# Attention followed by a quantised conv block: small products cut in halves, loads for the next block moved, and a count moved between conv bands

## The chip, the cores and the metric

One core of a Trainium2 chip runs one program. The metric is the device time of that program in microseconds, from its first to its last instruction, the median of several runs. All engine, line and tile names are those of the profile: PE is the matmul unit (TensorE), DVE is VectorE, ACT is ScalarE, POOL is GpSimd, SP is SyncE, which here only issues transfers.

## The reference

The input x has 4 images of 128 channels and 64 x 64 pixels, in float32. Two layers follow one another:

```python
# layer 0: attention over the 4096 pixels of an image, 4 heads of 32 channels
x_norm = group_norm(x, norm_w, norm_b)                      # 8 groups
qkv = einsum('oc,bchw->bohw', qkv_w, x_norm) + qkv_b
q, k, v = heads(qkv)                                        # [4, 4, 4096, 32] each
attn = softmax(einsum('bhid,bhjd->bhij', q, k) * 32**-0.5)
out = einsum('bhij,bhjd->bhid', attn, v)
x = x + einsum('oc,bchw->bohw', proj_w, out) + proj_b
# layer 1: two 3x3 convolutions with 3-bit weights, batch norm over all images
out = relu(batchnorm(conv3x3(x, lsq_quantize(w1, alpha1))))
out = batchnorm(conv3x3(out, lsq_quantize(w2, alpha2)))
x = relu(out + x)
```

## The kernel before

**Blocks and steps.** The attention runs as 32 blocks, `n` from 0 to 31: image `b` = n // 8 and a chunk `qb` = n % 8 of 512 queries. A block takes 32 steps `kt`, each over 128 keys. A step's scores are two pairs of heads; a pair (L418, tile s, two PSUM banks, three such tiles in turn) is four matmuls, and ACT takes its exponential (L420) into the tile p, of which there are eight. `weights` (L431) multiplies p by v into the accumulator acc (four matmuls, which the profile counts as eight; so are those of the small products). The sum of p over the keys, needed for softmax, is gathered by DVE (L441, L443) into r for 26 of the 32 steps; for the steps 4, 9, 14, 19, 24 and 28 (`MOVED`) a transfer of POOL adds p into rm instead (L436, L438), and one more adds rm to r (L464, `merge`).

**Order of the work.** It is written out by hand. The loop alternates a short phase (three pairs of scores, then one step of weights) and a long phase (three pairs, then two steps); both make a period of three steps. Every engine runs its instructions in that order. After the weights of step kt, `side(kt)` emits the tasks that `schedule(n, before)` has put at kt or earlier. `slots` lists the steps of a block that end a short phase: every third, 10 or 11 a block.

**Small products.** These are the tasks that use TensorE: for the next image, the projections k, q and v of a 512-pixel chunk j (`project_parts`, products pk, pq, pv at L301); for the block before, the sums l (`total`, L460) and the output projection po (L301). Each fills one PSUM bank of the pool `psa`. That pool has two buffers and acc holds one of them, so a small product can begin only when the one before it has been emptied. pk and pq are emptied by ACT (L331) and then DVE (L332), which split the value in two parts in a staging tile; POOL then writes that tile to DRAM (L336). pv is emptied by DVE (L350), l by ACT (L468), po by DVE (L516). In the first block the projections of image 0 that aren't made ahead of the loop are tasks too: 16 products in steps 0 to 23, in short and in long phases.

**The end of a block.** `merge`, `sums` (l), `spread`, `invert`, `gather`, `weigh` and `project` follow one another in the next block: l is copied to SBUF, row sums are spread over partitions by a transfer (lq), DVE inverts them (rq, L496), a transfer writes them to DRAM (rd) and another broadcasts them (rc), DVE multiplies (`weigh`, L506), TensorE projects (po), DVE adds the residual x (`store`, L516) and POOL writes y.

**Loads.** SP issues, in program order, the loads of x chunks (L230, three buffers), of q for the next block (L398, eight transfers, two buffers), of k and v for the next image (L387, L391, in the last quarter block of an image), and the transfers lq, rd and rc. In a block with qb = 1 the statistics for the next image's group norm are taken: eight x chunks are loaded at steps 0, 2, ... 14 and DVE runs bn_stats (L628) three steps later; then come the small products gm, gv and gb with DVE work between them (`norm_parts`).

**The convolutions** (`conv`, L701) run over 16 bands of 16 rows, each as 2 x 18 products from a high and a low part of the input (`split_band`, DVE, L541 and L542). ACT copies a result from PSUM to cv (L761) and DVE takes bn_stats of the copy (L762). Ahead of band 2 the kernel counts sums that were too large: two DVE instructions (L724, L726), a product of one column (nbad, L728) and a copy to cnt (L729).

Of the kernel before, what the change touches and what calls it, by code (L numbers as in the profile page):

```python
# [78 lines left out]
def _fast_body(ctx, tc, x, norm_w, norm_b, qkv_wt, qkv_b, proj_wt, proj_b,  # L79
# [223 lines left out]
    def project_parts(b, j, xin, start=False):  # L303
# [19 lines left out]
        def mm(what, o):  # L323
            ps[what] = bank(what)
            banded(ps[what], norm[b][0][:, o : o + P], xin())
# [12 lines left out]
        def mmv():  # L338
            ps["v"] = bank("v")
            for i in range(KB):  # L340
                banded(ps["v"][:, i * P : (i + 1) * P], xin()[:, i * P : (i + 1) * P],
                       norm[b][0][:, 2 * P : 3 * P])

        def evac_v():
# [8 lines left out]
            if b > 0:  # L353
                nc.gpsimd.dma_start(out=vd[b, j], in_=v)

        return [lambda: mm("k", P), lambda: parts("k", 0, kd),
                lambda: mm("q", 0), lambda: parts("q", 1, qd), mmv, evac_v]
# [87 lines left out]
    def finish_parts(n):  # L445
# [10 lines left out]
        def total(r, first, end):  # L456
            if first:
                t["l"] = psa.tile([P, FB], F32, name=f"l{n}", tag="a")
            for h in range(HEADS):
                nc.tensor.matmul(t["l"][h * D : (h + 1) * D, :], ones, r[:, h, :],  # L460
                                 start=first, stop=end)
# [8 lines left out]
        def sums():  # L470
            total(rsum[n], True, True)
            evacuate()
# [93 lines left out]
    def first_chunk(j, what, start):  # L566
        fs = project_parts(0, j, lambda: halves[j // 4][:, j % 4, :], start)
        i = 2 * "kqv".index(what)
        return fs[i : i + 2]
# [13 lines left out]
    late = {}  # L583

    def schedule(n, before):
        b, qb = blocks[n]
        todo = []
        slots = [kt for kt in range(NK - 1) if (n * NK + kt) % 3 == 0]

        def add(kt, f):  # L590
            todo.append((kt, f))

        if before:
            add(1, before["merge"])
            kt = slots[3]
            add(kt, before["sums"])
            add(kt + 1, before["spread"])
            add(kt + 3, before["invert"])
            add(kt + 4, before["gather"])
            add(kt + 6, before["residual"])  # L600
            add(kt + 11, before["weigh"])
            add(slots[8], before["project"])
            add(slots[8] + 1, before["store"])
        if n + 1 < len(blocks) and qb < NB - 1:
            add(14, lambda: load_q(b, qb + 1))
        if b + 1 < B and qb == NB - 1:
            add(24, lambda: load_q(b + 1, 0))

        def chunk(kts, fs):
            for i, kt in enumerate(kts):  # L610
                add(kt, fs[2 * i])
                add(kt + 1, fs[2 * i + 1])

        if n == 0:
            for kt, what, j in ((0, "v", 3), (2, "q", 1), (3, "k", 4), (5, "q", 2), (6, "k", 5),
                                (8, "q", 3), (9, "k", 6), (11, "v", 4), (12, "k", 7), (14, "v", 5),
                                (15, "v", 6), (17, "v", 7), (18, "q", 4), (20, "q", 5),
                                (21, "q", 6), (23, "q", 7)):
                chunk((kt,), first_chunk(j, what, False))
                if what == "k":  # L620
                    add(kt + 2, lambda j=j: load_k(0, j))
        if b + 1 < B:
            if qb == 1:
                st = small.tile([P, NB, 6], F32, name=f"st{b + 1}", tag="st")
                xs = {}
                for j in range(NB):
                    add(2 * j, lambda j=j: xs.update({j: load_x(b + 1, j)}))
                    add(2 * j + 3, lambda j=j: nc.vector.bn_stats(st[:, j, :], xs[j]))  # L628
                late[b] = norm_parts(b + 1, st)
                add(18, late[b][0])  # L630
                chunk((slots[7], slots[9]), late[b][1:5])
            if qb == 2:
                chunk(slots[0:1], late[b][5:7])
            for j, i in {2: ((0, (1, 2, 4)), (1, (5, 6, 7))), 3: ((2, (1, 2, 4)), (3, (5, 6, 7))),
                         4: ((4, (4, 5, 6)),), 5: ((5, (4, 5, 6)),), 6: ((6, (4, 5, 6)),),
                         7: ((7, (4, 5, 6)),)}.get(qb, ()):
                xt = {}
                kts = [slots[i] for i in i]
                add(max(kts[0] - 8, 0), lambda j=j, xt=xt: xt.update({0: load_x(b + 1, j)}))
                chunk(kts, project_parts(b + 1, j, lambda xt=xt: xt[0]))  # L640
# [81 lines left out]

    big = small.tile([P, 1], F32, name="big")
    nc.vector.tensor_reduce(big, worst, AX.X, ALU.max)  # L724
    bad = small.tile([P, 1], F32, name="bad")
    nc.vector.tensor_scalar(bad, big, LIMIT, None, ALU.is_gt)  # L726
    nbad = psa.tile([P, FB], F32, name="nbad", tag="a")
    nc.tensor.matmul(nbad[0:1, 0:1], bad, ones[:, 0:1], start=True, stop=True)  # L728
    nc.vector.tensor_copy(cnt, nbad[0:1, 0:1])  # L729
# [19 lines left out]
    def layer(i, prepare, done):  # L749

        st = mid.tile([P, B * NB, 6], F32, name=f"st{i}")
        for m, (b, g) in enumerate(bandlist):
# [5 lines left out]
            for j in range(2):  # L758
                c = 2 * g + j
                dst = cv[b][:, c * FB : (c + 1) * FB]  # L760
                nc.scalar.copy(dst, ps[:, j, :])  # L761
                nc.vector.bn_stats(st[:, b * NB + c, :], dst)  # L762
        return batch_norm(i, st)

    def first(m):
        if m + 3 < len(bandlist):
            load_band(*bandlist[m + 3])
# [513 lines left out]
```

## Time and profile before

| | us |
|---|---|
| time, median of 3 | 2655.54 (2654.3 to 2663.69) |
| span of the profiled run | 2654.6 |
| first scores to the first copy av<-acc (block 0) | 29.8 to 141.7 |
| block 1, copy to copy | 79.4 |
| block 9, copy to copy | 82.4 |
| last copy av<-acc, end of the attention | 2329.8 |

The copies av<-acc (L453), one at the end of each block, mark the blocks in time. Work of the engines in some blocks, from the stretches that these copies bound (us busy):

| stretch | PE | DVE | ACT |
|---|---|---|---|
| 29.8 to 141.7 (block 0) | 91.17 | 66.97 | 70.66 |
| 141.7 to 221.1 (block 1) | 70.46 | 62.56 | 60.40 |
| 715.3 to 797.8 (block 9) | 71.42 | 63.57 | 63.10 |
| 575.6 to 646.4 (block 7) | 69.34 | 60.49 | 61.86 |
| 2265.0 to 2329.8 (block 31) | 64.80 | 60.27 | 57.47 |

A row of the groups reads: line, engine, operation, output<-input with their shapes, count, then busy time and mean ns of one, then the time for which the engine stood idle ahead of them and what ended it. In the chain of waits each row is a start, a length and the work (or transfer) that the end was waiting for at that moment.

### The profile page before, as it was taken

The numbers are of one execution on the slowest core, as the hardware profiler recorded it, in microseconds if no ns is written. First come the engines' busy times: TensorE is split into PE (matmuls) and PEld (weight loads), VectorE is DVE, ScalarE is ACT, GpSimd is POOL, SyncE is SP. The second block draws the span as 40 slices with busy tenths as digits, with TensorE's granted clock in tenths as the row PEclk, the third lists the DMA queues.
The fourth block names the chain that finished last, engine by engine and source line by source line (L and its number), as shares of the span: only waits on it lengthen the run. The fifth ranks groups of instructions, "written<-read, shape, count | busy, mean of one in ns | idle before, by whom it ended". The sixth has DMA issues, their size and how long they took to land.

```text
span 2654.6 us, 46871 instructions
## 1 busy us (share of the span) xinstructions
PE 2543.2 (96%) x19634; PEld 1193.5 (45%) x19634; DVE 2134.9 (80%) x1402; ACT 2075.5 (78%) x2275; POOL 282.1 (11%) x456
## 2 busy tenths in 40 slices
PE   5889999999989999999999999999999999999995
PEld 2334444444434444443444444444444444467773
DVE  4678889888878888888988888878999999954334
ACT  3678888888878888888888888888898989911223
POOL 2101111111001111111011111110001001000000
PEclk9999999999999999999999999999999999999997
DMA  4765666778766666678766766796656667744004
GB/s 156 179 147 140 164 157 156 163 185 203 164 137 164 175 153 154 153 192 190 166 152 173 170 160 164 157 224 148 140 126 150 138 140 152 142 85 148 0 0 160
DMA packets 147411, 399.94 MB, mean 151 GB/s; under 512 B 59240, under 2 KB 60008, under 8 KB 118648
## 3 DMA queue, kind: packets, MB, share of 16 engines
q0 software_dynamic: 45888, 280.59, 46.3%
q1 hardware_dynamic: 100728, 115.23, 16.8%
q8 instruction: 156, 2.56, 0.4%
q10 hardware_dynamic: 576, 1.05, 0.1%
q14 instruction: 63, 0.52, 0.1%
HBM read 105.32 MB, written 55.83 MB: 61 GB/s over the span
## 4 chain that ended last, share of the span: by engine, by line
PE 85%; DMA 6%; issue 3%; DVE 2%; ACT 1%; POOL 0%; SPq 0%; POOLq 0%; ACTq 0%; DVEq 0%
PE s L418 38%; PE acc L431 33%; PE c L701 9%; DMA rm<-p 3%; DMA q<-qd 1%; PE l L460 1%; DVE r L443 1%; PE po L301 1%; PE pq L301 1%; PE pk L301 1%; PE pv L301 1%; DMA x<-in_x_dram 1%; DVE res L819 0%; ACT p L420 0%; DMA v<-vd 0%
## 5 line engine op out<-in xcount | busy, mean ns | idle before, releaser
L420 ACT ACTIVATE p<-s 128x1024 f32<-128x1024 f32 x2048 | 1932.0, 1034 | 302.0 <-PE s L418 228.1
L443 DVE TENSOR_TENSOR r<-r,p 128x2048 f32<-128x2048 f32 x768 | 1758.1, 2289 | 118.0 <-ACT p L420 72.7
L418 PE MATMUL s<-q,k 64*128 64x512 f32 x8192 | 1181.1, 416 | 12.4 <-ACT p L420 4.5
L418 PEld LDWEIGHTS s<-q,k 64*128 64x128 f32 x8192 | 709.2, 186 | 734.7 <-ACT p L420 322.6
L431 PE MATMUL acc<-p,v 128*32 128x512 f32 x8192 | 1023.6, 602 | 0.0
L431 PEld LDWEIGHTS acc<-p,v 128*32 128x32 f32 x8192 | 197.6, 109 | 456.0 <-issue 451.7
L438 POOL DMA_DIRECT2D rm<-p x160 | 139.3, 871 | 912.0 <-ACT p L420 674.6
L761 ACT COPY cv<-c 128x512 f32<-128x512 f32 x64 | 34.3, 590 | 223.8 <-PE c L701 210.8
L762 DVE BATCH_NORM_STATS2 st<-cv 128x6 f32<-128x512 f32 x64 | 41.2, 685 | 154.9 <-ACT cv L761 154.9
L701 PE MATMUL c<-hi,wq 128*128 128x512 f32 x576 | 151.4, 408 | 6.6 <-DVE hi L780 6.6
L701 PE MATMUL c<-lo,wq 128*128 128x512 f32 x576 | 148.0, 401 | 0.0
L701 PEld LDWEIGHTS c<-hi,wq 128*128 128x128 f32 x576 | 110.4, 192 | 38.0 <-issue 8.7
L701 PEld LDWEIGHTS c<-lo,wq 128*128 128x128 f32 x576 | 108.7, 189 | 29.1
L441 DVE TENSOR_TENSOR r<-p,p 128x2048 f32<-128x2048 f32 x32 | 73.3, 2290 | 42.9 <-ACT p L420 42.6
L332 DVE SCALAR_TENSOR_TENSOR kst<-pk,b,kst 128x512 fp32r<-128x512 f32 x32 | 24.0, 751 | 81.5 <-ACT kst L331 81.4
L332 DVE SCALAR_TENSOR_TENSOR qst<-pq,b,qst 128x512 fp32r<-128x512 f32 x32 | 24.0, 749 | 39.3 <-ACT qst L331 39.3
L464 POOL DMA_DIRECT2D r<-rm x31 | 26.3, 849 | 240.1 <-DMA rm<-p 108.4
L628 DVE BATCH_NORM_STATS2 st<-x 128x6 f32<-128x512 f32 x24 | 16.5, 687 | 32.9 <-DMA x<-in_x_dram 32.9
L336 POOL DMA_DIRECT2D kd<-kst x28 | 20.8, 744 | 205.3 <-DVE kst L332 191.0
L336 POOL DMA_DIRECT2D qd<-qst x31 | 23.1, 745 | 183.3 <-DVE qst L332 183.1
L436 POOL DMA_DIRECT2D rm<-p x32 | 17.8, 556 | 225.6 <-ACT p L420 140.0
L517 POOL DMA_DIRECT2D y<-x x32 | 18.5, 577 | 195.3 <-DVE x L516 195.3
(129 smaller groups left out, 660.1 us busy)
## 6 DMA issues: line engine op xcount, KB each, us to landing
rm<-p POOLq DMA_DIRECT2D x192, 1024.0 KB, 7.6
q<-qd SPq DMA_DIRECT2D x248, 128.0 KB
r<-rm POOLq DMA_DIRECT2D x31, 1024.0 KB, 7.0
x<-in_x_dram SPq DMA_DIRECT2D x80, 256.0 KB
k<-kd SPq DMA_DIRECT2D x124, 128.0 KB
qd<-qst POOLq DMA_DIRECT2D x31, 512.0 KB, 4.5
kd<-kst POOLq DMA_DIRECT2D x28, 512.0 KB, 6.1
y<-x POOLq DMA_DIRECT2D x32, 256.0 KB, 3.2
```

The source lines that it names most:

```text
L301: nc.tensor.matmul(out[cs, :], w[:, cs], x, start=True, stop=True)
L332: nc.vector.scalar_tensor_tensor(lo, ps[what], bias, t[:, 0, :], ALU.add, ALU.subtract)
L336: (nc.sync if start else nc.gpsimd).dma_start(out=dst[b, j].rearrange("s p n -> p s n"), in_=t)
L418: nc.tensor.matmul(s[:, i, :], k[r, half, c0 : c0 + P], q[r, half, part, :], start=(part == 0), stop=(part == 1))
L420: nc.scalar.activation(pts[step][:, 2 * half : 2 * half + 2, :], s, AF.Exp, scale=SCALE)
L431: nc.tensor.matmul(acc[n][h * D : (h + 1) * D, :], v[:, kt % KB, h * D : (h + 1) * D], pt[:, h, :], start=(kt == 0), stop=(kt == NK - 1))
L438: nc.gpsimd.dma_start(out=msum[n], in_=pt, accum_op=ALU.add)
L441: nc.vector.tensor_tensor(rsum[n], pts[step - 1], pt, ALU.add)
L443: nc.vector.tensor_tensor(rsum[n], rsum[n], pt, ALU.add)
L701: nc.tensor.matmul(ps[:, j, :].rearrange("p (r w) -> p r w", w=W), w[:, tap, :], part[:, j * RB + kh : j * RB + kh + RB, kw : kw + W], sta ...
L761: nc.scalar.copy(dst, ps[:, j, :])
L762: nc.vector.bn_stats(st[:, b * NB + c, :], dst)
```

## The change

- The small products k, q, v and l are cut in two halves of 256 columns. A helper `visit` puts the halves at the two slots that it is given (or both at one slot, as one product in two parts) and the emptying one step after the second. In blocks with one chunk, k goes to slots 0 and 1, l to 3 and 4, q to 5 and 6, v to 7 and 8; po moves from slot 8 to slot 9, and weigh to two steps ahead of it. In blocks with two chunks (qb 2 and 3) only the second v is cut.
- In the first block ten products are left, most of them three steps apart; six q products move to block 1.
- The x chunks for the statistics are loaded every one and a half steps, the x chunk of a block's first projection in the block before (step 22), and q for the next block is always loaded at step 14, across images too.
- The count of bad sums moves from ahead of band 2 to band 5, and bn_stats in the conv layers reads the result in PSUM, before the copy.

It is meant to spread the small products over the short phases, and to keep loads clear of what waits for them.

```diff
--- before.py
+++ after.py
@@ -320,9 +320,13 @@
                 t = stage.tile([P, n, FB], F32, name=f"{what}st{b}_{j}", tag=tag)
             return t
 
-        def mm(what, o):
-            ps[what] = bank(what)
-            banded(ps[what], norm[b][0][:, o : o + P], xin())
+        halves = [slice(i * FB // 2, (i + 1) * FB // 2) for i in range(2)]
+        def mm(what, o, i):
+            if i == 0:
+                ps[what] = bank(what)
+            cs = halves[i]
+            banded(ps[what][:, cs], norm[b][0][:, o : o + P], xin()[:, cs])
 
         def parts(what, o, dst):
             t = staged(2, what)
@@ -335,9 +339,10 @@
             else:
                 (nc.sync if start else nc.gpsimd).dma_start(out=dst[b, j].rearrange("s p n -> p s n"), in_=t)
 
-        def mmv():
-            ps["v"] = bank("v")
-            for i in range(KB):
+        def mmv(i):
+            if i == 0:
+                ps["v"] = bank("v")
+            for i in range(i * KB // 2, (i + 1) * KB // 2):
                 banded(ps["v"][:, i * P : (i + 1) * P], xin()[:, i * P : (i + 1) * P],
                        norm[b][0][:, 2 * P : 3 * P])
 
@@ -353,8 +358,10 @@
             if b > 0:
                 nc.gpsimd.dma_start(out=vd[b, j], in_=v)
 
-        return [lambda: mm("k", P), lambda: parts("k", 0, kd),
-                lambda: mm("q", 0), lambda: parts("q", 1, qd), mmv, evac_v]
+        return dict(k=(lambda: mm("k", P, 0), lambda: mm("k", P, 1), lambda: parts("k", 0, kd)),
+                    q=(lambda: mm("q", 0, 0), lambda: mm("q", 0, 1), lambda: parts("q", 1, qd)),
+                    v=(lambda: mmv(0), lambda: mmv(1), evac_v))
 
 
     def k_tile(b, j):
@@ -453,11 +460,11 @@
             nc.scalar.copy(av, acc[n])
 
 
-        def total(r, first, end):
-            if first:
+        def total(r, first, end, cs=slice(0, FB)):
+            if "l" not in t:
                 t["l"] = psa.tile([P, FB], F32, name=f"l{n}", tag="a")
             for h in range(HEADS):
-                nc.tensor.matmul(t["l"][h * D : (h + 1) * D, :], ones, r[:, h, :],
+                nc.tensor.matmul(t["l"][h * D : (h + 1) * D, cs], ones, r[:, h, cs],
                                  start=first, stop=end)
 
         def merge():
@@ -467,9 +474,10 @@
             t["ls"] = stage.tile([P, FB], F32, name=f"ls{n}", tag="ls")
             nc.scalar.copy(t["ls"], t["l"])
 
-        def sums():
-            total(rsum[n], True, True)
-            evacuate()
+        def sums(i):
+            total(rsum[n], True, True, slice(i * FB // 2, (i + 1) * FB // 2))
+            if i == 1:
+                evacuate()
 
 
         def sums_at_once():
@@ -564,9 +572,7 @@
         f()
 
     def first_chunk(j, what, start):
-        fs = project_parts(0, j, lambda: halves[j // 4][:, j % 4, :], start)
-        i = 2 * "kqv".index(what)
-        return fs[i : i + 2]
+        return project_parts(0, j, lambda: halves[j // 4][:, j % 4, :], start)[what]
 
     def load_kv(b, j):
         load_k(b, j)
@@ -580,64 +586,79 @@
 
 
 
-    late = {}
+    late, xin = {}, {}
+    def fetch(b, j):
+        xin[b, j] = load_x(b, j)
 
...
         slots = [kt for kt in range(NK - 1) if (n * NK + kt) % 3 == 0]
+        two = b + 1 < B and qb in (2, 3)
+        full = two or n == 1
 
         def add(kt, f):
             todo.append((kt, f))
 
+        def visit(kts, first, second, evacuate=None):
+            add(kts[0], first)
+            add(kts[-1], second)
+            if evacuate:
+                add(kts[-1] + 1, evacuate)
         if before:
             add(1, before["merge"])
-            kt = slots[3]
-            add(kt, before["sums"])
+            kts = slots[3:4] if full else slots[3:5]
+            visit(kts, lambda: before["sums"](0), lambda: before["sums"](1))
+            kt = kts[-1]
             add(kt + 1, before["spread"])
             add(kt + 3, before["invert"])
             add(kt + 4, before["gather"])
             add(kt + 6, before["residual"])
-            add(kt + 11, before["weigh"])
-            add(slots[8], before["project"])
-            add(slots[8] + 1, before["store"])
-        if n + 1 < len(blocks) and qb < NB - 1:
-            add(14, lambda: load_q(b, qb + 1))
-        if b + 1 < B and qb == NB - 1:
-            add(24, lambda: load_q(b + 1, 0))
-        def chunk(kts, fs):
-            for i, kt in enumerate(kts):
-                add(kt, fs[2 * i])
-                add(kt + 1, fs[2 * i + 1])
+            add(slots[9] - 2, before["weigh"])
+            add(slots[9], before["project"])
+            add(slots[9] + 1, before["store"])
+        if n + 1 < len(blocks):
+            add(14, lambda: load_q(*blocks[n + 1]))
         if n == 0:
-            for kt, what, j in ((0, "v", 3), (2, "q", 1), (3, "k", 4), (5, "q", 2), (6, "k", 5),
-                                (8, "q", 3), (9, "k", 6), (11, "v", 4), (12, "k", 7), (14, "v", 5),
-                                (15, "v", 6), (17, "v", 7), (18, "q", 4), (20, "q", 5),
-                                (21, "q", 6), (23, "q", 7)):
-                chunk((kt,), first_chunk(j, what, False))
+            for kt, what, j in ((0, "k", 4), (2, "q", 1), (3, "v", 3), (6, "k", 5), (9, "k", 6),
+                                (12, "v", 4), (15, "k", 7), (18, "v", 5), (21, "v", 6),
+                                (24, "v", 7)):
+                visit((kt,), *first_chunk(j, what, False))
                 if what == "k":
                     add(kt + 2, lambda j=j: load_k(0, j))
+        if n == 1:
+            for i, j in zip((0, 1, 2, 4, 5, 6), range(2, NB)):
+                visit(slots[i : i + 1], *first_chunk(j, "q", False))
         if b + 1 < B:
             if qb == 1:
                 st = small.tile([P, NB, 6], F32, name=f"st{b + 1}", tag="st")
-                xs = {}
                 for j in range(NB):
-                    add(2 * j, lambda j=j: xs.update({j: load_x(b + 1, j)}))
-                    add(2 * j + 3, lambda j=j: nc.vector.bn_stats(st[:, j, :], xs[j]))
+                    add(3 * j // 2, lambda j=j: fetch(b + 1, j))
+                    add(3 * j // 2 + 3, lambda j=j: nc.vector.bn_stats(st[:, j, :], xin[b + 1, j]))
                 late[b] = norm_parts(b + 1, st)
-                add(18, late[b][0])
-                chunk((slots[7], slots[9]), late[b][1:5])
+                add(15, late[b][0])
+                for i in (0, 1):
+                    add(slots[7 + i], late[b][1 + 2 * i])
+                    add(slots[7 + i] + 1, late[b][2 + 2 * i])
             if qb == 2:
-                chunk(slots[0:1], late[b][5:7])
-            for j, i in {2: ((0, (1, 2, 4)), (1, (5, 6, 7))), 3: ((2, (1, 2, 4)), (3, (5, 6, 7))),
-                         4: ((4, (4, 5, 6)),), 5: ((5, (4, 5, 6)),), 6: ((6, (4, 5, 6)),),
-                         7: ((7, (4, 5, 6)),)}.get(qb, ()):
-                xt = {}
-                kts = [slots[i] for i in i]
-                add(max(kts[0] - 8, 0), lambda j=j, xt=xt: xt.update({0: load_x(b + 1, j)}))
-                chunk(kts, project_parts(b + 1, j, lambda xt=xt: xt[0]))
+                add(slots[0], late[b][5])
+                add(slots[0] + 1, late[b][6])
+            chunks = {1: (), 2: (0, 1), 3: (2, 3), 4: (4,), 5: (5,), 6: (6,), 7: (7,)}
+            for i, j in enumerate(chunks.get(qb, ())):
+                p = project_parts(b + 1, j, lambda j=j: xin[b + 1, j])
+                if not two:
+                    places = dict(k=slots[0:2], q=slots[5:7], v=slots[7:9])
+                elif i == 0:
+                    places = dict(k=slots[1:2], q=slots[2:3], v=slots[4:5])
+                else:
+                    places = dict(k=slots[5:6], q=slots[6:7], v=slots[7:9])
+                    add(8, lambda j=j: fetch(b + 1, j))
+                for what, kts in places.items():
+                    visit(kts, *p[what])
+            if qb > 0 and qb + 1 in chunks:
+                add(22, lambda j=chunks[qb + 1][0]: fetch(b + 1, j))
             if qb == NB - 1:
                 for j in range(NB - 1):
                     add(4 * j + 1, lambda j=j: load_kv(b + 1, j))
@@ -719,14 +740,6 @@
     last["project"]()
     last["store"]()
     split_band(*bandlist[2])
-    big = small.tile([P, 1], F32, name="big")
-    nc.vector.tensor_reduce(big, worst, AX.X, ALU.max)
-    bad = small.tile([P, 1], F32, name="bad")
-    nc.vector.tensor_scalar(bad, big, LIMIT, None, ALU.is_gt)
-    nbad = psa.tile([P, FB], F32, name="nbad", tag="a")
-    nc.tensor.matmul(nbad[0:1, 0:1], bad, ones[:, 0:1], start=True, stop=True)
-    nc.vector.tensor_copy(cnt, nbad[0:1, 0:1])
     att.close()
 
     mid = ctx.enter_context(tc.tile_pool(name="mid", bufs=1))
@@ -758,11 +771,23 @@
             for j in range(2):
                 c = 2 * g + j
                 dst = cv[b][:, c * FB : (c + 1) * FB]
+                nc.vector.bn_stats(st[:, b * NB + c, :], ps[:, j, :])
                 nc.scalar.copy(dst, ps[:, j, :])
-                nc.vector.bn_stats(st[:, b * NB + c, :], dst)
         return batch_norm(i, st)
 
+    def count_bad():
+        big = small.tile([P, 1], F32, name="big")
+        nc.vector.tensor_reduce(big, worst, AX.X, ALU.max)
+        bad = small.tile([P, 1], F32, name="bad")
+        nc.vector.tensor_scalar(bad, big, LIMIT, None, ALU.is_gt)
+        nbad = psa.tile([P, FB], F32, name="nbad", tag="a")
+        nc.tensor.matmul(nbad[0:1, 0:1], bad, ones[:, 0:1], start=True, stop=True)
+        nc.vector.tensor_copy(cnt, nbad[0:1, 0:1])
     def first(m):
+        if m == 5:
+            count_bad()
         if m + 3 < len(bandlist):
             load_band(*bandlist[m + 3])
         if m + 2 < len(bandlist) and m > 0:
```

## The prediction

> **What bounds the kernel now.** I read the busy table first, then the total waits, then the timeline of one ordinary stretch, then the chain of waits in the stretches that run long. The busy table:
>
> ```profile
> PE 2543.2 (96%) x19634; PEld 1193.5 (45%) x19634; DVE 2134.9 (80%) x1402; ACT 2075.5 (78%) x2275; POOL 282.1 (11%) x456
> ```
>
> TensorE sets the end, so the question is which of its gaps the change closes. An ordinary stretch of block 5 in the timeline (start, length, engine, line; TensorE alone):
>
> ```profile
> 556.27 1.67 PE L418 MATMUL s<-q,k 64*128 64x512 f32 x12
> ...
> 558.75 1.04 PE L301 MATMUL po<-av,wp 128*32 128x512 f32 x8
> ...
> 559.72 1.66 PE L418 MATMUL s<-q,k 64*128 64x512 f32 x12
> ...
> 563.17 1.67 PE L418 MATMUL s<-q,k 64*128 64x512 f32 x12
> ...
> 565.76 1.82 PE L418 MATMUL s<-q,k 64*128 64x512 f32 x12
> ...
> 569.37 1.66 PE L418 MATMUL s<-q,k 64*128 64x512 f32 x12
> ```
>
> Every L418 row opens a phase of three score pairs. The short phase has one step of L431 after them, the long phase two. With a small product (po) in the short phase a period is 559.72 - 556.27 = 3.45 plus 563.17 - 559.72 = 3.45, so **6.90 us**. Without one it is 2.59 + 3.61 = **6.20 us**. The product costs 0.70 and not its own 0.86 (3.45 - 2.59), because an empty short phase is paid back: its 2.59 is less than ACT's three exponentials (2.86 on their row), and the next long phase waits for PSUM (3.61 against 3.45). That wait, in total, and two others:
>
> ```profile
> PEld s L418 <- ACT p L420: 322.6, 492, 2.6
> ...
> PE gm L249 <- DVE mv L244: 33.1, 3, 13.6
> ...
> DVE st L628 <- DMA x<-in_x_dram: 32.9, 3, 15.0
> ```
>
> The copies av<-acc (L453), one a block, show which blocks run long: about 66 us in image 3, 69 to 74 with projections, but 79.4 in block 1 and 82.4 in block 9, and block 0 has 111.9 from its first scores to its copy. The chain in block 1:
>
> ```profile
> 171.46 5.85 DMA rd<-rq
> 177.31 0.02 issue
> 177.32 0.59 SPq L503
> 177.91 0.06 issue
> 177.97 0.03 SPq L398
> 178.00 0.04 issue
> 178.04 6.58 DMA q<-qd
> 184.62 0.02 issue
> 184.63 9.02 DMA x<-in_x_dram
> 193.65 0.02 issue
> 193.67 0.04 DVE st L628
> ```
>
> The last x chunk for the statistics is issued behind eight q loads on SyncE's queue; VectorE sits in bn_stats until it lands, and TensorE sits in the gm product. In block 0 the timeline shows another wait: products come one and a half steps apart, through one free psa bank, and each waits until VectorE has emptied it:
>
> ```profile
> 53.42 1.06 PE L301 MATMUL pq<-xh,wn 128*32 128x512 f32 x8 [1.52 <-DVE kst L332]
> ...
> 59.46 1.72 PE L301 MATMUL pk<-xh,wn 128*32 128x512 f32 x8 [2.39 <-DVE qst L332]
> ```
>
> **What the Trainium skill says.** (1) "TensorE: Matmul & The Clock Gate", section Back-to-back issue gap: for wide products the time goes with the columns streamed. The trace agrees: pv is 16 products of 128 columns and occupies 25.4/24 = 1.06 us a chunk, pk is 4 of 512 and occupies 25.0/24 = 1.04. So I price half a product at half of 0.86. (2) Same page, section What's actually happening: an idle window of about 3.4 us drops the clock to half. Agreed: after 3.4 us of idle before the nbad product the next nine matmuls take 3.86 us, against 2.3 elsewhere. (3) "DMA: Bandwidth & Descriptors", section Issuing engines are not separate DMA queues: all transfers share 16 engines. The rm<-p additions, which GpSimd issues, land in 6.9 to 15.2 us here, so moving q loads can slow them. (4) "PSUM — Partial Sum Buffer", section PSUM bank collisions raise a hardware error: two engines must not touch a bank at once; no run shows it yet, but it means the new bn_stats and the copy take turns.
>
> **The change, part by part.**
> - *Halves.* 12 blocks (quarters 4 to 7 of images 0 to 2) halve k, q and v: 36. Six full blocks halve the second v: 6. The l product is halved in 31 - 7 = 24 blocks. That is 66. A product and an empty period cost 6.90 + 6.20 = 13.10 now. In halves a short phase is 2.59 + 0.43 = 3.02, more than 2.86, so the long phase needs no wait: 2 x (3.02 + 3.45) = 12.94. 0.16 to 0.18 each, **-11**. Against it: weigh now comes two steps ahead of the po product, not four. Between them TensorE has about 4.3 us (two weights steps, three pairs, one step); an addition (2.29), weigh (0.69) and v's evacuation (0.68) make 3.7 plus VectorE's lag, which over the additions at steps 25 to 27 has medians of 0.2 to 1.1 us. Some po products wait 0.3 us or so, and block boundaries where store now comes one step before the next acc also: +2. Net **-9**.
> - *Block 0.* 16 products become 10, all but one in short phases three steps apart. The stalls beyond the phases' own work, summed over that window by comparing each phase with ordinary ones, are 27 us after the pipeline has filled. k4 at step 0, q1 at 2, v3 at 3 still crowd: two waits of 2 to 3 us remain. **-22**. Six q products leave (6 x 0.86 = **-5.2**) for block 1. v5 is now made two steps ahead of its use; its evacuation needs one addition and 0.68 us within 4.3 us, so I cost it at nothing. The k staging tile is rewritten 6.9 us apart while its write lands in 6.1 after GpSimd's issue: a wait of about 1 us on ACT, inside its 0.59 of slack a phase.
> - *Block 1.* It gets the six q products (+5.2) and loses the wait of 14 us on x. TensorE then has about 71.5 us. VectorE has 62.6 busy now and gets six evacuations of 0.75: 67, denser in its first half, so it lags. I take 74 against 79.4: **-5.4**.
> - *Blocks 9 and 17.* The loads come at 0, 1, 3 ... 10 with the last bn_stats at 13, ahead of the q loads. Block 9 loses 14 us to its wait and falls to about 70: **-12.5**. Block 17 loses 2.6 now: **-1**. The gather of rc is now issued behind the q loads there and in other blocks; it has from step 14 to weigh at 25 to 27, some 25 us, for q loads (5.5 to 13.4), rd (5.85 with its issue) and rc itself. Hidden.
> - *Image boundaries.* q of the next image is loaded at step 14, not 24. Phases at these three boundaries lose 14.6 us in all; the 6.4 in block 23 are a wait on that load (DMA q<-qd 9.01 in its chain), the rest mostly on rm<-p additions, which stay. **-6**.
> - *Count of bad sums.* TensorE idles 3.4 us before nbad. Band 2's hi is ready at 2351.64, nbad ran at 2353.48: 1.9 saved, and without so long a gap the slow nine matmuls give up to 1.5. bn_stats from PSUM takes turns with the copy: the tail of a layer goes from 1.9 to about 2.1 us, twice. **-3**.
>
> Sum: -9 - 22 - 5.2 - 5.4 - 12.5 - 1 - 6 - 3 = -64.1, so 2655.5 - 64.1 = 2591.
>
> **Rivals.** *A: only the removed waits pay.* Halves give nothing since po and ACT's evacuations (0.70 in a phase with 0.59 of slack) take it back, boundaries stay, block 1 becomes VectorE's: -22 - 5.2 - 3 - 12 - 1 = -43, 2612. For it: VectorE is at 93% in blocks with projections; against it: those blocks show no wait on it now. *B: everything is recovered.* 27 + 12.9 + 14.3 + 2.6 of stalls in blocks 0, 1, 9 and 17, 14.6 at boundaries, 11 for halves, 4 at the bands: -86, 2569. Against it: the crowd at steps 0 to 3 and the rm<-p chain remain. *C: a new wait replaces the old one, and it ends slower.* If rc, rd or lq lands behind the q loads too late, VectorE stops at weigh or invert as it stops at bn_stats now, but in some 22 blocks. At 5 us each that is +110 against -64: 2700. Against it: 25 us of room against at most 22.
>
> **How the numbers follow.** Forecast 0.62, A 0.22, B 0.11, C 0.05. The forecast's own terms are uncertain by about 12 us together, A's centre is 2612 and B's 2569; 2575 to 2617 leaves out C, half of B and the upper third of A, some 2 in 10. Slower is C without its mild form, 0.04; mild forms of C give no change, 0.03; faster 0.93.
>
> **What would show it.** Right: block 0 near 85 us from its first scores to its copy, no wait of bn_stats on x, blocks 1 and 9 at 74 and 70, periods of 6.47 us with 256-column products, TensorE's wait on ACT in L418 down by a third, and no 3.4 us gap ahead of band 2. Wrong: halves that last over 0.5 us, waits of po on VectorE over 1 us, waits of VectorE at weigh or invert on DMA, or a longer rm<-p chain in blocks 7, 15 and 23.

## The result and the profile after

| | before | after |
|---|---|---|
| time, us (median) | 2656.65 (4 runs) | 2589.17 (2588.28 to 2592.37, 4 runs) |
| ratio | | 0.9744, interval 0.9723 to 0.9765 |
| span of the profiled run, us | 2654.6 | 2588.2 |
| first scores to the copy, block 0 | 111.9 | 85.8 |
| block 1 / block 9 | 79.4 / 82.4 | 74.3 / 69.8 |

Since one copy av<-acc ends each block, two profiles can be subtracted block by block. In blocks that an edit doesn't touch the length repeats within 0.3 us from run to run, mostly within 0.1, except for the lead-in and block 0 (up to 2.6 us together), block 1 (up to 1.9) and, now and then, one of 16 to 28 (up to 1.6); from the last copy to the end it repeats within 0.8. The table sets the prediction's terms against these differences.

| term of the prediction | predicted | measured, us |
|---|---|---|
| block 0 (waits, and six q products gone) | -27.2 | -26.9 at its copy |
| block 1 | -5.4 | -5.1 |
| block 9 / block 17 | -12.5 / -1 | -12.7 / -1.1 |
| boundaries (7, 8, 15, 16, 23), beyond halves | -6 | -12.9 |
| halves, gross | -11 | -11.6 |
| what the halves' layout costs (weigh, store) | +2 | +6.4 in blocks 25, 26 and 28 |
| convolutions | -3 | -2.6 |
| sum | -64.1 | -66.4 |

The row of the halves is a remainder: what the blocks that no other row names lost (9.2), with 2.4 added for the halves in the five boundary blocks.

The busy line of the page after: TensorE is busy for a larger share of a shorter span.

```profile
PE 2517.2 (97%) x20394; PEld 1223.4 (47%) x20394; DVE 2140.3 (83%) x1402; ACT 2081.9 (80%) x2275; POOL 281.4 (11%) x456
```

The timeline of block 4 after, TensorE's rows that open a phase, and the half product pk between them (L425 is what L418 was):

```profile
411.35 1.67 PE L425 MATMUL s<-q,k 64*128 64x512 f32 x12
413.83 0.62 PE L301 MATMUL pk<-x,wn 128*32 128x256 f32 x8
414.37 1.66 PE L425 MATMUL s<-q,k 64*128 64x512 f32 x12
417.81 1.67 PE L425 MATMUL s<-q,k 64*128 64x512 f32 x12
420.41 1.89 PE L425 MATMUL s<-q,k 64*128 64x512 f32 x12
```

A short phase with a half lasts 3.02 us and the long one behind it 3.44: together 6.46, and the prediction worked out 6.47. The row at 417.81 opens an empty short phase (2.60), and the scores that follow at 420.41 are stretched to 1.89 by the wait for PSUM. The total waits after:

```profile
PEld s L425 <- ACT p L427: 209.2, 376, 2.0
...
PE gm L249 <- DVE mv L244: 13.6, 1, 13.6
...
PEld po L301 <- DVE av L514: 8.5, 5, 3.4
```

The wait of the scores on ACT is down from 322.6 us, by a third; the one wait of gm that is left is image 0's, ahead of all blocks; bn_stats (L639) waits for x no more. New is the last line: po waits for weigh. In block 0 the timeline still shows the crowd of its first three steps:

```profile
41.29 1.07 PE L301 MATMUL pq<-xh,wn 128*32 128x256 f32 x16 [1.52 <-DVE kst L336]
...
47.33 1.25 PE L301 MATMUL pv<-wn,xh 128*32 128x128 f32 x32 [2.38 <-DVE qst L336]
```

The second of these waits costs more than its 2.38 us. A row of the next view is a stretch and its length, then the busy time of PE, PEld, DVE, ACT and POOL, TensorE's granted clock (1.00 is full) and the load of the transfers. Two pairs of stretches after the change, in block 0 and in block 26:

```profile
44.70:48.11 3.41, 1.03 (x32) 0.78 (x32) 1.81 (x2) 1.79 (x3) 0.54 (x1) 1.00 0.48 151
48.11:51.52 3.41, 3.41 (x28) 2.02 (x24) 1.39 (x2) 1.76 (x2) 0.76 (x2) 0.50 0.89 334
1918.62:1922.03 3.41, 0.89 (x12) 0.16 (x8) 3.41 (x3) 1.12 (x2) 0.00 (x0) 1.00 1.03 204
1922.03:1925.44 3.41, 3.41 (x20) 1.94 (x20) 3.31 (x2) 1.72 (x2) 0.00 (x0) 0.50 0.33 67
```

and two neighbouring ones before it, in block 0:

```profile
42.67:46.08 3.41, 2.33 (x20) 0.91 (x16) 1.88 (x1) 2.97 (x4) 0.00 (x0) 1.00 0.48 170
46.08:49.49 3.41, 2.11 (x18) 1.09 (x20) 0.75 (x1) 0.80 (x2) 1.29 (x2) 1.00 0.44 156
```

After the change the wait of 2.38 us lies within one stretch, and the next 3.41 us run at half the clock: twelve scores take 2.93 us and not 1.67. Before it a wait of the same length (45.00 to 47.38) is cut at 46.08 into 1.08 and 1.30 us, and the clock stays at 1.00. In each of the 14 traces the half-clock stretches, as they are called below, begin whole multiples of 3.41 us apart. Cut on that grid from 31 us on, every stretch at full clock in which TensorE stood idle for more than 1.9 us was followed by a half-clock one, none with less than 1.4 us was, and between the two both occur. So what a wait costs depends on where it falls. This is most of what doesn't repeat in blocks 1, 26 and 28: block 26 takes 70.4 us in the five runs in which a half-clock stretch follows its wait, and 68.9 in the two in which the same wait has none. Before the change 41 us of the attention ran at half clock (blocks 0, 1, 9 and 23), after it 6.8 (blocks 0 and 26). TensorE was busy for 28.9 and 6.8 us of that, and half of the difference, some 11 us of the 66, is clock rather than waiting (an estimate from these traces).

At the bands TensorE waits for hi (L549) and no longer for the count. The nine products last 2.43 us, not 3.86; first before, then after:

```profile
2353.48 0.19 PE L728 MATMUL nbad<-ones,bad 128*1 128x1 f32 x2 [3.35 <-DVE bad L726]
2353.60 3.86 PE L701 MATMUL c<-hi,wq 128*128 128x512 f32 x9
```

```profile
2287.93 2.43 PE L722 MATMUL c<-hi,wq 128*128 128x512 f32 x9 [1.56 <-DVE hi L549]
```

### The profile page after: what moved, and what is told of

It is laid out like the page before. It is cut to its first block, busy times and chain, and to the rows that moved or that the text cites. A ratio compares the mean times of both kernels' runs of the same rounds, so it can differ in the third digit from the quotient of the medians.

```text
span 2588.2 us, 48399 instructions
## 1 busy us (share of the span) xinstructions
PE 2517.2 (97%) x20394; PEld 1223.4 (47%) x20394; DVE 2140.3 (83%) x1402; ACT 2081.9 (80%) x2275; POOL 281.4 (11%) x456
## 4 chain that ended last, share of the span: by engine, by line
PE 88%; DVE 5%; issue 3%; DMA 2%; ACT 1%; POOL 0%; SPq 0%; DVEq 0%; POOLq 0%; ACTq 0%
PE s L425 39%; PE acc L438 34%; PE c L722 9%; DVE r L450 3%; DMA rm<-p 2%; PE l L467 1%; PE po L301 1%; PE pk L301 1%; PE pq L301 1%; PE pv L301 1%; ACT p L427 1%; DVE res L844 1%; DMA xh<-in_x_dram 0%; DMA q<-qst 0%; DVE st L570 0%
## 5 line engine op out<-in xcount | busy, mean ns | idle before, releaser
L425 PE MATMUL s<-q,k 64*128 64x512 f32 x8192 | 1162.3, 413 | 3.9 <-ACT p L427 2.2
L425 PEld LDWEIGHTS s<-q,k 64*128 64x128 f32 x8192 | 711.7, 185 | 631.9 <-issue 298.0
L774 DVE BATCH_NORM_STATS2 st<-c 128x6 f32<-128x512 f32 x64 | 44.7, 699 | 124.5 <-PE c L722 102.5
L722 PEld LDWEIGHTS c<-lo,wq 128*128 128x128 f32 x576 | 109.0, 189 | 28.9
L335 ACT ACTIVATE kst<-pk,b 128x512 fp32r<-128x512 f32 x32 | 22.4, 701 | 21.7 <-PE pk L301 21.7
L467 PE MATMUL l<-r,ones 128*32 128x256 f32 (+1 forms) x504 | 37.9, 383 | 0.5 <-issue 0.5
```

What stands on the lines that cost most here:

```text
L425: nc.tensor.matmul(s[:, i, :], k[r, half, c0 : c0 + P], q[r, half, part, :], start=(part == 0), stop=(part == 1))
L467: nc.tensor.matmul(t["l"][h * D : (h + 1) * D, cs], ones, r[:, h, cs], start=first, stop=end)
L722: nc.tensor.matmul(ps[:, j, :].rearrange("p (r w) -> p r w", w=W), w[:, tap, :], part[:, j * RB + kh : j * RB + kh + RB, kw : kw + W], sta ...
L774: nc.vector.bn_stats(st[:, b * NB + c, :], ps[:, j, :])
```

## The experiments

All are edits of the changed kernel except the one that says otherwise. Differences are against the changed kernel's profile.

**Halves made whole.**

```diff
-            add(kts[-1], second)
-            if evacuate: add(kts[-1] + 1, evacuate)
+            add(kts[0], second)
+            if evacuate: add(kts[0] + 1, evacuate)
```

> The changed kernel, but every product that is cut over two slots is made whole at the first of them; all other tasks stay where they are. Theory (an empty short phase costs a wait of about 0.17 us in the next long phase, and halves fill it): each of the 66 products costs 0.16 to 0.18 us more, so blocks 4 to 6, 12 to 14 and 20 to 22 are longer by 0.5 to 0.7 us each, TensorE's wait on ACT at the scores rises by a third again, and the time is 9 to 11 us over the changed kernel, 2598 to 2600. Rival (the shorter blocks come from loads that are issued earlier): those blocks stay as they are, within 0.2 us, and the time stays at 2589.

Measured: 2610.97 us. The nine blocks named are longer by 0.67 to 0.77 each, as the theory has it, and the scores' wait on ACT is

```profile
PEld s L425 <- ACT p L427: 257.1, 407, 3.6
```

So a half in an empty short phase is worth what the period arithmetic says. That wait rose by 23%, though, not by the third that was expected, and the time rose by twice the forecast. The boundaries took another 9.3 us beyond the halves' own share (block 8 +3.4, block 23 +4.9), and block 0 with its lead-in 2.6, of the size in which that repeats; 3.7 came back in blocks 25, 26 and 28. The boundaries thus depend on where the products stand too: in block 23 of this run an addition rm<-p of 14.2 us holds ACT, and with it the scores.

**weigh four steps ahead of po.**

```diff
-            add(slots[9] - 2, before["weigh"])
+            add(slots[9] - 4, before["weigh"])
```

> The changed kernel, with weigh four steps ahead of the po product again and not two. Theory (the 4.3, 2.0 and 0.7 us that blocks 26, 28 and 25 lose are po waiting for weigh, which stands in VectorE's queue behind the weight pieces of those blocks): these waits go, block 26 falls to 66, and the time is 6 to 7 us under the changed kernel, 2582 to 2583. Rival (VectorE is simply late in those blocks, and TensorE would wait for it somewhere else): the loss moves to another product or to the p tiles, and the time stays within 2 us of 2589.

Measured: 2588.72 us, the same. The waits named did go: blocks 25, 26 and 28 are shorter by 0.7, 4.2 and 2.0. But block 27 is longer by 2.6, blocks 29 and 30 by 0.4 and 0.5, and block 1 by 1.8, since its wait of 1.8 us is followed by a half-clock stretch in this run. Block 26 got back its wait of 2.5 us and, with it, the half-clock stretch. Two timelines show the exchange, first the changed kernel in block 26, then this run at the start of block 27:

```profile
1920.54 0.69 DVE L514 TENSOR_TENSOR av<-av,rc 128x512 f32<-128x512 f32 x1
...
1921.28 1.25 PE L301 MATMUL po<-av,wp 128*32 128x512 f32 x8 [2.52 <-DVE av L514]
```

```profile
1928.83 0.74 DVE L524 SCALAR_TENSOR_TENSOR x<-po,bp,x 128x512 f32<-128x512 f32 x1
...
1929.63 1.07 PE L438 MATMUL acc<-p,v 128*32 128x512 f32 x8 [2.71 <-DVE x L524]
```

po no longer waits for weigh. The next block's acc now waits for store, which empties po's bank and stands in the same late queue of VectorE. Theory and rival were each half right.

**Fewer weight pieces in a block**, then the same with weigh four steps ahead.

```diff
-        if b == B - 1 and 0 < qb < NB - 1:
-            for kt in range(1, NK - 1, 5):
+        if b == B - 1 and qb < NB - 1:
+            for kt in range(1, NK - 1, 6):
```

> The changed kernel, with VectorE's weight pieces of the last image spread over seven blocks (24 to 30, five in each) and not six (25 to 30, six in each); weigh stays two steps ahead of po. Theory (po waits in blocks 25, 26 and 28 since weigh comes late in VectorE's queue, which lags because the pieces fill it): the lag of the additions grows less, and of the 7 us lost in these blocks 3 to 6 come back, 2583 to 2586. Rival (two steps are too few for weigh in any case): the same loss, perhaps in other blocks, 2589.

> The run before this one, with weigh four steps ahead of po as well. Theory: weigh alone moved the wait from block 26 to block 27 because VectorE was still late; with fewer pieces a block and weigh earlier no block of 24 to 30 waits over 1 us, and the time is 5 to 7 us under the changed kernel, 2582 to 2584. Rival (VectorE's work in the last image sets its time): the blocks 24 to 30 sum to the same as with weigh alone, some 3 us under the changed kernel.

Measured: 2587.83 and 2585.80 us. With the pieces spread, block 26 is 3.9 and block 28 1.9 shorter, block 25 0.4 longer, and no other block of the image pays: 5.3 us come back with weigh still two steps ahead, within the 3 to 6 expected. With both, blocks 24 to 30 sum to 6.2 us less (25 -0.7, 26 -4.2, 27 +0.5, 28 -2.0), about twice what weigh alone gave. It was VectorE's lateness that made two steps too few. The whole time shows less than that and misses both forecasts of it, since block 0's copy came 1.3 and 1.9 us later in these two runs. Against the kernel before the last one has a ratio of 0.9727 (0.9714 to 0.9741); the interval overlaps the changed kernel's, so it is faster than the kernel before, and faster than the changed one only by its blocks.

**q of the next image at step 24.**

```diff
-            add(14, lambda: load_q(*blocks[n + 1]))
+            add(24 if qb == NB - 1 else 14, lambda: load_q(*blocks[n + 1]))
```

> The changed kernel, with q of the next image loaded at step 24 of an image's last block again and not at 14; three blocks are touched. The boundaries (blocks 7, 8, 15, 16, 23) became 12.8 us shorter beyond what halves explain, where 6 was forecast. Theory 1 (the early load alone, since it also keeps the rm<-p additions of steps 24 and 28 clear of the q transfers): the time rises by about 12, to 2601, and blocks 7, 8 and 15 lose 2 us each again. Theory 2, the forecast's (only the wait on q in block 23 goes back): it rises by 6, in block 23 alone.

Measured: 2606.28 us (2603.82 to 2612.24). The profile is of the longest of the four executions; in it blocks 7, 8, 15, 16 and 23 are longer by 9.8, 1.7, 4.5, 0.7 and 5.2, which is 21.9, where the median time rose by 17.1. The chain at the end of block 7:

```profile
595.43 11.77 DMA v<-vd
607.20 0.02 issue
607.21 9.89 DMA q<-qd
617.11 0.04 issue
617.15 2.07 PE s L425 x7
```

The scores of the next block wait for q, and q waits behind v. Half-clock stretches follow these waits; TensorE is busy in them for 17.3 us, so that some 9 of the 21.9 are clock (an estimate, half of that). Both theories were too small: block 7 had lost nothing to q in the kernel before.

**The kernel before, with q of the next image at step 14.**

```diff
-        if n + 1 < len(blocks) and qb < NB - 1:
-            add(14, lambda: load_q(b, qb + 1))
-        if b + 1 < B and qb == NB - 1:
-            add(24, lambda: load_q(b + 1, 0))
+        if n + 1 < len(blocks):
+            add(14, lambda: load_q(*blocks[n + 1]))
```

> The kernel before with one edit: q of the next image is loaded at step 14 of an image's last block and not at 24. Theory (this load alone keeps the boundaries long): blocks 7, 8, 15, 16 and 23 fall by what they fell in the changed kernel beyond the halves, 1.7, 2.5, 2.7, 0.4 and 5.5 us, the other blocks stay, and the time is 11 to 13 us under the kernel before. Rival (the early load helps only together with halves and the other moves, which leave the rm<-p additions more room): only block 23's wait on q goes, 5 to 6 us.

Measured: 2659.83 against 2659.55 us, ratio 1.0003 (0.9994 to 1.0012). Against the kernel before, blocks 7, 8, 15 and 23 change by -0.9, +3.0, +0.6 and -1.8. In block 8 a half-clock stretch follows the wait in this run and not in the kernel before. Both numbers fall: the early load alone gives nothing. The rival's reason, that it helps only together with the other moves, is what is left. The chain through blocks 7 and 8, first of this run, then of the kernel before:

```profile
616.58 13.86 DMA rm<-p
...
630.99 9.75 DMA rm<-p
...
641.29 11.69 DMA rm<-p
```

```profile
618.19 12.62 DMA rm<-p
...
631.36 11.95 DMA rm<-p
...
643.86 10.28 DMA rm<-p
```

The additions of p by transfer follow one another almost without a gap, the first of them issued behind the writes of kst and qst on GpSimd's queue, and at the end ACT waits for p tiles. Here the edit finds no wait on q to remove. In block 23, where the kernel before waits for q, the edit removes that wait, and an addition of 14.2 us holds ACT in its place. With k, q and v at neighbouring slots these writes come in a bunch; in the changed kernel they are spread over the block. Which of the spread's effects frees the additions was not tried alone; that products made whole bring one of these waits back is seen in the first run.

**x for the statistics every two steps.**

```diff
-                    add(3 * j // 2, lambda j=j: fetch(b + 1, j))
-                    add(3 * j // 2 + 3, lambda j=j: nc.vector.bn_stats(...))
-                add(15, late[b][0])
+                    add(2 * j, lambda j=j: fetch(b + 1, j))
+                    add(2 * j + 3, lambda j=j: nc.vector.bn_stats(...))
+                add(18, late[b][0])
```

> The changed kernel, with the eight x chunks of the statistics loaded every two steps again (the last one at step 14, in the same step as the eight q loads and behind them), bn_stats three steps later and its aggregate at step 18. Theory (the last x waits behind the q loads on SyncE's queue, and bn_stats stops VectorE): blocks 1 and 9 lose 9 to 14 us each again, block 17 up to 3, and the time is 20 to 28 us over the changed kernel, 2609 to 2617. Rival (what mattered was VectorE's load in the first half of the block): a few us at most.

Measured: 2607.10 us. Block 1 is 14.4 us longer, but block 9 only 0.2 and block 17 not at all. The theory held in one block of three. In block 9 the order on SyncE had changed in another way; its issues (SPq) in that stretch:

```profile
721.61 0.56 SPq L500 DMA_DIRECT2D lq<-ls  x1
722.23 6.85 SPq L405 DMA_DIRECT2D q<-qd  x8
...
729.18 0.62 SPq L230 DMA_DIRECT2D x<-in_x_dram  x1
729.89 0.88 SPq L506 DMA_DIRECT2D rd<-rq  x1
```

Here the q loads go out ahead of rd and gather, because l is made in halves and ends a period later; in block 1 l is whole.

**The same, with l whole in blocks 1, 9 and 17.**

```diff
-        full = two or n == 1
+        full = two or (qb == 1 and b + 1 < B)
```

> As the run with x loads every two steps, and in the blocks with statistics (1, 9, 17) the l product is whole at its first slot, so that spread, invert and gather come a period earlier and the q loads are issued behind gather, as in the kernel before; block 1 has had that order in all runs. Theory (the q loads, and x behind them, are late when SyncE first waits for rd and gather; in block 9 it was the later l product, not the earlier x loads, that took this order away): block 9 is 9 to 13 us longer than in the run with x loads every two steps (70), block 17 by 0 to 3. Rival (block 9 is cured for another reason): it stays at 70.

Measured: 2623.01 us. Block 9 is 13.0 us longer than in the changed kernel, block 17 1.4. Its chain is that of the kernel before:

```profile
719.29 1.40 DMA rd<-rq
720.70 0.02 issue
720.71 0.54 SPq L511
721.25 0.04 issue
721.29 13.81 DMA q<-qd
735.11 0.02 issue
735.12 9.58 DMA x<-in_x_dram
```

So in block 9 the later l is enough without the earlier x. That the earlier x is enough without the later l was run in block 1 alone, where l is whole in the changed kernel; in block 9 it is likely but not shown, and a later l was not tried in block 1.

**x every two steps, with q at step 20.**

```diff
+            add(20 if qb == 1 and b + 1 < B else 14, lambda: load_q(*blocks[n + 1]))
```

> As the one before (x loads every two steps, the last at step 14), but in the blocks with statistics q for the next block is loaded at step 20, behind all x loads. Theory (the order against the q loads on SyncE's queue is what counts, not the pace of the x loads): the wait on x goes, blocks 1, 9 and 17 are within 1.5 us of the changed kernel's 74, 70 and 67, and the time is 2589 to 2592. Rival (loads at this pace are too late for bn_stats and the group norm products behind it in any case): blocks 1 and 9 stay long as in the run before, 2609 or more.

Measured: 2598.25 us. Block 1 is 5.6 us longer than in the changed kernel, not 14.4; blocks 9 and 17 are unchanged. The order against q explains most of block 1's wait. The rest is still a wait on x, behind gather this time, with a half-clock stretch of 6.8 us after it:

```profile
152.79 0.59 SPq L511
...
153.44 13.66 DMA x<-in_x_dram
```

**The first block's order of before.**

```diff
-            for kt, what, j in ((0, "k", 4), (2, "q", 1), (3, "v", 3), (6, "k", 5), ...):
+            for kt, what, j in ((0, "v", 3), (2, "q", 1), (3, "k", 4), (5, "q", 2), ...):
-        if n == 1:   # six q products
```

> The changed kernel, with the first block's order of before: 16 products there, every one and a half steps, and none of the six q products in block 1. Theory (one free bank, so each product waits until ACT and VectorE have emptied the one before): block 0 is 27 us longer again, at 112 from its first scores to its copy, block 1 is 4 to 6 us shorter without the q products, at 68 to 70, and the time is 21 to 23 us over the changed kernel, 2610 to 2612. Rival (block 0 is bound by the engines' work and by transfers, the order matters little): block 0 grows by the 5.2 us of the six products alone and block 1 shrinks by as much, 2589.

Measured: 2609.65 us. Block 0's copy comes 24.6 us later and block 1 is 7.0 shorter. The waits are back at twelve of the 16 products, 18.2 us in all against 3.9 in the changed kernel. These 14.3 us more and the six products (5.2) make 19.5; the rest is about what three more half-clock stretches in block 0 cost, at half of 3.41 us each (an estimate from the trace). The rival, which has the two cancel, is out.

**The count ahead of band 2.**

```diff
     split_band(*bandlist[2])
+    count_bad()
     att.close()
...
-        if m == 5:
-            count_bad()
```

> The changed kernel, with the count of bad sums ahead of band 2 again. Theory: the product nbad holds TensorE until VectorE has made it, 1.9 us after band 2 is ready, and the longer gap slows the next nine products by 1.4: the gap between po and band 2 is 4.5 us again, the nine products take 3.8 and not 2.4, and the time is 3.3 us over the changed kernel, 2592. Rival (the gap is set by the split of band 2, the count hides beside it): no difference, 2589.

Measured: 2595.66 us. From the last copy to the end the profile is 3.5 us longer, which is the theory's 3.3; most of the rest lies in blocks 0 and 1 (+0.5 and +1.9), which this edit doesn't touch; in block 1 a half-clock stretch follows the wait. The nine products took 3.2 us rather than 3.8, and the nine behind them 3.1 rather than 2.3. TensorE at band 2:

```profile
2292.32 0.19 PE L738 MATMUL nbad<-ones,bad 128*1 128x1 f32 x2 [3.35 <-DVE bad L736]
2292.43 3.16 PE L722 MATMUL c<-hi,wq 128*128 128x512 f32 x9
```

**Three edits together**: weigh four steps ahead, v3 and k4 exchanged in the first block, bn_stats from the copy.

```diff
+            add(slots[9] - 4, before["weigh"])
+            for kt, what, j in ((0, "v", 3), (2, "q", 1), (3, "k", 4), (6, "k", 5), ...):
+                nc.scalar.copy(dst, ps[:, j, :])
+                nc.vector.bn_stats(st[:, b * NB + c, :], dst)
```

> The changed kernel with three edits: weigh four steps ahead of po; in the first block v3 at step 0 and k4 at step 3 (v is emptied by VectorE alone, so q1 at step 2 doesn't wait for it); bn_stats of the conv layers from the copy again. Theory: 6 to 7 us from weigh, 2 to 2.5 from the first block (one wait of 2.7 us in place of 5.1 in its first phases), 0.3 from the tails of the conv layers, 2579 to 2581. Rival (losses move on, as in VectorE's queue): 2587 to 2590.

Measured: 2589.02 us, no gain. The three phases after the first are 15.3 us, against 17.0 in the changed kernel, so the exchange gives 1.7 there; the first phase took 8.4 and not 7.2, within what it varies in these runs (6.6 to 8.5). Of the 6.9 us that weigh gave, 3.0 were lost again in blocks 27 to 30, block 1 was 1.9 longer, with a half-clock stretch behind its wait, and the convolutions showed no gain (+0.7 from the last copy on). The total is the rival's, though here the losses moved on only in part; the rest is the clock.

## Why the prediction was right, and where only its sum was right

**Block 0**: the step held to 0.3 us, closer than block 0 repeats, so the last digits are luck. The first block's order and the move of the six products make it (+24.6 when undone). The two waits left are the ones named, 1.5 and 2.4 us rather than 2 to 3 each. What the step called stalls is waits and the slow clock behind them together.

**Block 1**: right in size. The wait on x was removed by the early x loads, as the runs with x at two steps show. Of its 14 us TensorE stood idle for 8.4, and 10.2 us at half clock came with it. What keeps the block at 74 and not at 71.5 is not mainly VectorE's lag, as the prediction had it, but an addition of p by transfer that lands late, issued behind a write of qst on GpSimd's queue, while ACT waits 2.1 us for a p tile and TensorE 1.6. The chain there:

```profile
160.36 14.58 DMA rm<-p
```

**Block 9**: right in size, incomplete in cause. The prediction named only the loads "ahead of the q loads"; here the later l removes the wait by itself.

**Halves**: 11.6 for 11, and the mechanism is shown by the periods and by the run with whole products. The cost of weigh and store was mis-sized: +2 predicted, +6.4 measured. The step that failed took VectorE's lag from medians over blocks 2 to 30. The cost sits in blocks 25, 26 and 28 of the last image, where the weight pieces fill VectorE: the addition ahead of weigh starts 2.0, 4.1 and 3.3 us after the start of its step's product on TensorE, and po waits 0.5, 2.5 and 1.8 us; the half-clock stretch in block 26 adds the rest. The prediction also put VectorE's 93% in the wrong place. In the kernel before it is busy for 82 to 89% of the blocks with projections, and for 95 to 97% of blocks 25 to 29, which have none.

**Boundaries**: -6 predicted, -12.9 measured. The step "a wait on that load (...), the rest mostly on rm<-p additions, which stay" failed in its last two words: the additions recovered as well. Neither the early q load alone (0) nor the changed kernel without it gives this: with q at step 24 its five boundary blocks are no shorter than in the kernel before (6.7 us longer in the profiles). Both are needed, and which of the change's other moves the early load needs stays open. The 6.4 us that the prediction put down to a wait in block 23 are 2.8 us of idle time and a stretch of 6.8 us at half clock, which cost about half of its length.

**Convolutions**: right. The count's part is shown by undoing it (+3.5). That bn_stats and the copy take turns is seen in the waits, since ACT's copies wait for bn_stats 64 times of 64; the gap ahead of the second convolution is 6.77 us with bn_stats first and 6.62 with the copy first, of the size of the 0.2 predicted and too little to show in the time.

The two mis-sized terms were off by -6.9 and +4.4 us and partly cancel, so that the total is closer than its parts: that is luck. Rival A's claim that halves give nothing is refuted by the phases; C's waits on rc, rd or lq stayed small (VectorE waited 9.3 us in all on lq, 2.2 at most). C's own chances don't add up: 0.04 for slower and 0.03 for no change are more than its 0.05.

## What to carry to other kernels

Read what a small task costs from the period that holds it, with and without, not from its own duration: where an empty phase is paid back by another engine's wait, half the task in each of two phases is cheaper than the whole in one. In a queue that one engine issues in order, ask for each load what stands ahead of it and what that waits for. Read the granted clock behind each of TensorE's waits before pricing it: here a wait of 2.4 us cost 2.4 or about 4. A median of a lag hides the blocks in which another task fills the same engine; and a wait removed from one reader of a late queue goes to the next reader unless the queue itself gets less work.

## What was not expected of the hardware

- bn_stats on 128x512 takes 699 ns when it reads PSUM and 685 when it reads SBUF.
- The prediction cites about 3.4 us of idle time ahead of the half clock, and its own case at nbad agreed. Here far less was enough: waits of 2.4 and 2.5 us, and in three runs one of 1.7 to 1.8 us in block 1, when they fell within one stretch of the 3.41 us grid. A wait of 3.17 us in the run with whole products, cut by the grid into 1.62 and 1.55, left the clock at 1.00.
- The 160 transfers that each add 1 MB landed in 6.9 to 14.6 us, median 8.2; the slowest stands in block 1. In the kernel before they took 6.9 to 15.2, median 8.1. What makes one of them slow was not tried.
